# Second attention of layer 1: its node part inside the first attention, one written order for both, norms behind each group

## The chip, the cores and the metric

The kernel runs on one core of a Trainium2 chip. The metric is the device time of one execution in microseconds. TensorE is called PE here, VectorE DVE, ScalarE ACT, GpSimd POOL and SyncE SP.

## The reference

A graph network of four layers over 3125 nodes with 256 features and 103125 edges. The change lies in layer 1, whose graph part has two attentions in a row, the first with four heads, the second with one:

```python
z = jnp.einsum('ni,hoi->nho', h, W1)
es = jnp.einsum('nho,ho->nh', z, a_s)
ed = jnp.einsum('nho,ho->nh', z, a_d)
e = _leaky(es[src] + ed[dst])
alpha = _segment_softmax(e, dst, n)
m = jax.ops.segment_sum(alpha[:, :, None] * z[src], dst, num_segments=n)
h1 = jax.nn.elu(m.reshape(n, HEADS * HID))
z2 = h1 @ W2.T
e2 = _leaky((z2 @ a2[:OUT_DIM])[src] + (z2 @ a2[OUT_DIM:])[dst])
alpha2 = _segment_softmax(e2, dst, n)
out = jax.ops.segment_sum(alpha2[:, None] * z2[src], dst, num_segments=n)
```

The result is added to `x`. Then come a layer norm of `x` and a feed-forward part with a shared network and four gated experts, added to `x` again.

## The kernel before

The edges are not gathered in this layer. Once, early on, the kernel counts how many edges go from each source to each destination and keeps that matrix as bytes (`count_d`). An attention is then a dense product: for a tile of 128 sources, a matrix `pt` of weights is made for a range of destinations, and PE multiplies it with the features `zs` of the sources, a column of ones among them for the softmax's denominator. There are `NS` = 25 source tiles of 128 (the last has 53) and `NT` = 25 destination tiles of `TP` = 125.

The weights come from one DVE instruction, `weigh` (L2066): the maximum of a row `q` of the destination and a scalar `bar` of the source, times the counts. The factor exp(es) of the source lies in `zs`, so the leaky rectifier needs no exponential per edge. The counts come on SP's queue (`count_tile`, L2073), in a ring of four buffers.

**First attention** (`dense`). The destinations are cut into chunks of 6, 6, 6 and 7 tiles. In a chunk, each source tile takes four weighs (one per head, 750 or 875 columns), 16 matmuls into `acc0` and `acc1` (L2321: pairs of heads, two PSUM banks each) and 8 for the sums into `acc2` (L2326). The `pt` ring has 7 buffers. After each source tile the loop runs one piece of side work, `next(work, None)`. Side work of a chunk is what the chunk before left behind: `turned` transposes the accumulators (L2279) and yields, then takes the inverse of the sums (L2285, L2286) and scales on ACT with an exponential for the ELU (L1121, L1123; from tile 18 on a part of it on DVE, L1125), and yields; `finish` (L1130) ends the ELU one tile later. `elu_turned` transposes the result into `xT` (L1141, L1142). Behind the last chunk all its side work runs alone.

The whole of `dense` is inside a manual schedule for PE, DVE and ACT: the instructions of these engines keep the order in which the program writes them. Outside such a block a planner orders each engine's instructions.

**Second attention** (`dense_one`, outside any manual schedule). First the node part, `node_pieces`: row products for `q` (L2012, L2013), and for each source tile two products of 257 columns, a copy by ACT into `zs` (L2027) and a copy by DVE of the source term (L2030). At the end come the exponentials of all source terms (L2032, L2036) and the scaling of all of `zs` (L2041). Then, for each of seven groups of destinations (`GROUPS`: four of 4 tiles, three of 3), 25 source tiles, with one weigh and 4 or 3 matmuls of 257 columns each (L2373), and three DVE instructions per destination tile that add the result to `x` (L2377 to L2379).

**Feed-forward** (`ffn1`). A layer norm per group (L632 to L644), which the planner places as soon as a group of `x` is ready, then for each group transposes of the normed rows into `xT` (`columns`, L294, L300, L302), the gate, and the two networks. Here PE's order alone is written by hand, in a table of steps.

Of the kernel before, what the change touches and what calls it, by code (L numbers as in the profile page):

```python
# [11 lines left out]
F32 = mybir.dt.float32  # L12
# [5 lines left out]
OP = mybir.AluOpType  # L18
# [40 lines left out]
def dview(ap, offset, dims):  # L59
    return bass.AP(tensor=ap.tensor, offset=ap.offset + offset, ap=[list(d) for d in dims])  # L60


class Net:
# [1104 lines left out]
        gw, gb = self.weight(c, "L1_ffn_gW"), self.row(c, "L1_ffn_gb")  # L1168
        return s1, s2, s3, sb1, sb2, e1, e2, e3, eb1, eb2, b3, own, gw, gb

    def ffn1(self, x, xn, xT, weights):
        nc, tc = self.nc, self.tc
        E = 4
        with ExitStack() as s:
# [9 lines left out]
                return nt * TP, slice(t0 * TP, (t0 + nt) * TP)  # L1184

            def columns(i):
                self.transposed(ps, xT, xn, groups=[GROUPS[i]])

            def gate(i):
                nt = GROUPS[i][1]  # L1190
# [54 lines left out]
                            + [(turns[i][:, ts], b3)])  # L1245
                    nc.vector.tensor_add(x[:, t0 + t, :], x[:, t0 + t, :], q)

            for g in GROUPS:
                self.layernorm(xn, x, g)
            steps = ((0, shared1), (1, lambda i: third(i, 0, 2)), (0, lambda i: first(i, 0)), (1, lambda i: third(i, 2, 4)), (0, turn),  # L1250
                     (0, shared2), (0, lambda i: second(i, 0)), (0, lambda i: first(i, 1)), (-1, columns), (0, lambda i: second(i, 1)), (-1, gate))
# [368 lines left out]
class Dense(Net):  # L1620
# [360 lines left out]
    def nodes(self, c, name, H):  # L1981

        HW = C + H
        return (c.tile([P, NS, HW + 31], F32, name="zs"), c.tile([P, NS, H], F32, name="bar"),
                self.dram.tile([H, N], F32, name="q_" + name))
# [57 lines left out]
            if h % 2:  # L2043
                yield

    def dense_nodes(self, c, name, xT, H, slope):
        nodes = self.nodes(c, name, H)
        with self.tc.tile_pool(name="dn", bufs=1) as w, self.tc.tile_pool(name="dnp", bufs=4, space=PSUM) as ps:
            for _ in self.node_pieces(nodes, name, xT, H, slope, w, ps):
                pass  # L2050
        return nodes

    def beside(self, c, name, xT, H, slope, mix, bias=None, gw=None):

        nodes = self.nodes(c, name, H)
# [199 lines left out]
                while ends:  # L2255
                    ends = [e for e in ends if next(e, self) is not self]

    def dense(self, nodes, scaled, then, finish=None, loops=False, early=None):


        nc, tc = self.nc, self.tc
# [1 line left out]
        W = D + 1  # L2263
        zs, bar, q_d = nodes
        with ExitStack() as s:
            wq = s.enter_context(tc.tile_pool(name="daq", bufs=6))
            wa = s.enter_context(tc.tile_pool(name="daa", bufs=4))
            wp = s.enter_context(tc.tile_pool(name="dap", bufs=7))
            wo = s.enter_context(tc.tile_pool(name="dao", bufs=1))
            ps1 = s.enter_context(tc.tile_pool(name="dap1", bufs=1, space=PSUM))  # L2270
            ps = s.enter_context(tc.tile_pool(name="dapp", bufs=2, space=PSUM))

# [20 lines left out]
            def ask(c, i0):  # L2293
                t0, nt = chunks[c]
                d0, n = t0 * TP, nt * TP
                for i in range(i0, i0 + 2):
                    q = wq.tile([P, 875], F32, name="q_head")
                    nc.scalar.dma_start(q[:, :n], dview(q_d, i * N + d0, [[0, P], [1, n]]))
                    queries.setdefault(t0, []).append(q)

            work = iter(())
            with tc.manual_schedule(engines={mybir.EngineType.PE, mybir.EngineType.DVE, mybir.EngineType.Activation}):
                for i in (0, 2):
                    ask(0, i)
                for c, (t0, nt) in enumerate(chunks):
                    d0, n = t0 * TP, nt * TP
                    half = (nt + 1) // 2
                    banks = [(0, half * TP), (half * TP, n)]
                    qs = queries.pop(t0)
                    acc = [ps1.tile([P, 2, 512], F32, name=f"acc{i}") for i in range(3)]  # L2310
                    for t in range(NS):
                        a, K = self.count_tile(wa, t, d0, n, loops)
                        pts = [self.weigh(wp, qs[i][:K, :n], bar[:K, t, i:i + 1], a, n, K) for i in range(4)]
                        st = dict(start=(t == 0), stop=(t == NS - 1))

                        for i0 in (0, 2):
                            for b, (b0, b1) in enumerate(banks):
                                for i in range(i0, i0 + 2):
                                    for f in (0, 32):
                                        r = 64 * (i % 2) + f  # L2320
                                        nc.tensor.matmul(acc[i // 2][r:r + 32, b, :b1 - b0], zs[:K, t, i * W + f:i * W + f + 32],  # L2321
                                                         pts[i][:K, b0:b1], **st)
                        for b, (b0, b1) in enumerate(banks):
                            for i in range(4):
                                z = i * W + D
                                nc.tensor.matmul(acc[2][32 * i:32 * i + 32, b, :b1 - b0],  # L2326
                                                 zs[:K, t, z:z + 32], pts[i][:K, b0:b1], **st)
                        if t == 12 and t0 + nt < NT:
                            ask(c + 1, 0)
                        next(work, None)  # L2330
                    for _ in work:
                        pass
                    if t0 + nt < NT:
                        ask(c + 1, 2)
                    os = []
                    for i, p in enumerate(acc):
                        o = wo.tile([P, 2, 512], F32, name=f"o{i}")
                        for b, (b0, b1) in enumerate(banks):
                            nc.scalar.activation(o[:, b, :b1 - b0], p[:, b, :b1 - b0], AF.Copy)
                        os.append(o)  # L2340
                    work = turned(os, t0, nt, half)
                    if t0 + nt < NT:
                        work = chain(work, then(t0, nt, ps))
                if early:
                    early(ps)
                for _ in work:
                    pass
                work = then(t0, nt, ps)
                if early:
                    return work  # L2350
                for _ in work:
                    pass

    def dense_one(self, x, name, xT, slope):

        nc, tc = self.nc, self.tc
        with ExitStack() as s:
            c = s.enter_context(tc.tile_pool(name="da", bufs=1))
            zs, bar, q_d = self.dense_nodes(c, name, xT, 1, slope)
            q = c.tile([P, N], F32, name="q_all")  # L2360
            nc.scalar.dma_start(q, dview(q_d, 0, [[0, P], [1, N]]))
            wa = s.enter_context(tc.tile_pool(name="daa", bufs=4))
            wp = s.enter_context(tc.tile_pool(name="dap", bufs=6))
            wo = s.enter_context(tc.tile_pool(name="dao", bufs=4))
            ps = s.enter_context(tc.tile_pool(name="dapp", bufs=2, space=PSUM))
            for t0, nt in GROUPS:
                d0, n = t0 * TP, nt * TP
                acc = [ps.tile([TP, C + 1], F32, name=f"acc{i}") for i in range(nt)]
                for t in range(NS):
                    a, K = self.count_tile(wa, t, d0, n, False)  # L2370
                    pt = self.weigh(wp, q[:K, d0:d0 + n], bar[:K, t, :], a, n, K)
                    for i in range(nt):
                        nc.tensor.matmul(acc[i], pt[:K, i * TP:(i + 1) * TP], zs[:K, t, :C + 1],  # L2373
                                         start=(t == 0), stop=(t == NS - 1))
                for i in range(nt):
                    inv = wo.tile([TP, 1], F32, name="inv")
                    nc.vector.tensor_scalar(inv, acc[i][:, C:], 1e-30, None, op0=OP.max)  # L2377
                    nc.vector.reciprocal(inv, inv)
                    nc.vector.scalar_tensor_tensor(x[:, t0 + i, :], acc[i][:, :C], inv, x[:, t0 + i, :],  # L2379
                                                   op0=OP.mult, op1=OP.add)  # L2380

# [674 lines left out]
    def run(self, x_in, out):  # L3058
# [1 line left out]
        self.setup_dense()  # L3060
        pool = self.ctx.enter_context(tc.tile_pool(name="x", bufs=1))
        x = pool.tile([TP, NT, C], F32, name="x")
        self.xn_all = pool.tile([P, NT, C], F32, name="xn")
        xn = self.xn_all[:TP]
        xT = pool.tile([P, KC, N], F32, name="xT")
        x_v = x_in.rearrange("(t p) c -> p t c", p=TP)
# [11 lines left out]
    def layers(self, x, xn, xT, out, late):  # L3078
        nc, tc = self.nc, self.tc
        xn_d = self.dram.tile([N, C], F32, name="xn_d")  # L3080
        with tc.tile_pool(name="hold", bufs=1) as hold:
# [21 lines left out]

                    y_d, (gw1, wkv) = self.routed0(x, xn, xT, xn_d, gate, weights, following)

            with tc.tile_pool(name="da", bufs=1) as c, tc.tile_pool(name="elu", bufs=2) as w:
                nodes = self.beside(c, "g1", xT, 4, 0.01, lambda work: self.mix1(x, xn, xT, work, (y_d, gate[-1]), wkv), gw=gw1)
                pre.close()
                minus = w.tile([P, 1], F32, name="minus", bufs=1)
                nc.gpsimd.memset(minus, -1.0)  # L3110
                scaled, finish = self.elu_parts(w, xn)
                self.dense(nodes, scaled, lambda t0, nt, ps: self.elu_turned(minus, xT, xn, t0, nt, ps), finish)
        with tc.tile_pool(name="ffn1", bufs=1) as wp:
            weights = self.ffn1_weights(wp)
            self.dense_one(x, "g1b", xT, 0.01)
            self.ffn1(x, xn, xT, weights)

        norms = self.ffn2_norms(late.enter_context(tc.tile_pool(name="bn2", bufs=1)))
        right = ExitStack()
# [155 lines left out]
```

## Time and profile before

| what | value |
|---|---|
| median of 3 runs | 5175.78 us (5175.36 to 5178.33) |
| the profiled execution | 5168.58 us |
| its span, first to last instruction | 5166.8 us |
| PE busy in the span | 4686.3 us, 91% |
| DVE | 3403.8 us, 66% |
| ACT | 1659.9 us, 32% |
| POOL | 1522.7 us, 29% |
| mean granted PE clock | 0.943 |
| first attention's weighs (and those of a later layer), L2066 on 750 or 875 columns | 773.3 us of DVE, 800 instructions |
| second attention's matmuls, L2373 | 276.1 us of PE, 1250 records |

Each time is from one profiled execution. A product of 32-bit numbers shows as two records on PE. Busy PE time is modelled from pipelined matmuls; idle time of an engine that limits nothing costs nothing. In the span the first attention of layer 1 begins at 1710.7 us; its last matmuls are issued at 2128.8, the first of the second attention start at 2195.2, its last end at about 2471, and the feed-forward ends at about 2662.

### The profile page before, as it was taken

The numbers are of one execution on the slowest core, as the hardware profiler recorded it, in microseconds if no ns is written. First come the engines' busy times: TensorE is split into PE (matmuls) and PEld (weight loads), VectorE is DVE, ScalarE is ACT, GpSimd is POOL, SyncE is SP. The second block draws the span as 40 slices with busy tenths as digits, with TensorE's granted clock in tenths as the row PEclk, the third lists the DMA queues.
The fourth block names the chain that finished last, engine by engine and source line by source line (L and its number), as shares of the span: only waits on it lengthen the run. The fifth ranks groups of instructions, "written<-read, shape, count | busy, mean of one in ns | idle before, by whom it ended". The sixth has DMA issues, their size and how long they took to land.

```text
span 5166.8 us, 74947 instructions
## 1 busy us (share of the span) xinstructions
PE 4686.3 (91%) x28167; PEld 2876.9 (56%) x28167; DVE 3403.8 (66%) x5802; ACT 1659.9 (32%) x2789; POOL 1522.7 (29%) x1414
## 2 busy tenths in 40 slices
PE   6898999969899899899999999999997788989878
PEld 4564433548656644388555333455664565555567
DVE  6987887755635899555334999622236887777743
ACT  2668877731343011200232011233331102333221
POOL 1107866814300000000001000000005777777733
PEclk8899999979999999899999999999998889999989
DMA  4866544531300111111000111200006566666645
GB/s 94 82 59 167 162 125 142 150 106 64 100 1 1 46 37 40 40 38 35 2 16 1 51 35 38 67 15 0 1 1 171 166 173 186 174 182 179 175 138 172
DMA packets 350161, 443.50 MB, mean 86 GB/s; under 512 B 144857, under 2 KB 269147, under 8 KB 349220
## 3 DMA queue, kind: packets, MB, share of 16 engines
q1 hardware_dynamic: 266674, 222.80, 17.9%
q0 software_dynamic: 55024, 175.53, 11.7%
q10 hardware_dynamic: 28095, 40.29, 2.5%
q8 instruction: 228, 3.74, 0.3%
q14 instruction: 140, 1.15, 0.1%
HBM read 384.87 MB, written 56.78 MB: 85 GB/s over the span
## 4 chain that ended last, share of the span: by engine, by line
PE 67%; DVE 11%; issue 6%; POOL 5%; ACT 4%; DMA 3%; SPq 0%; DVEq 0%; ACTq 0%; POOLq 0%
PE acc L2321 9%; PE p_tr L750 8%; PE acc L2373 5%; PE p_n L2161 5%; PE p_acc L2545 5%; PE acc L2326 4%; PE p_h L750 4%; PE p_y L750 4%; PE p_q L750 4%; POOL z_edge L2477 3%; PE p_f L2206 3%; PE p_a L750 3%; DVE pt L2066 2%; PE p_t L750 2%; PE p_kvt L750 2%
## 5 line engine op out<-in xcount | busy, mean ns | idle before, releaser
L2477 POOL DMA_INDIRECT z_edge<-tab,src_i x806 | 775.4, 962 | 268.4 <-issue 207.1
L2066 DVE SCALAR_TENSOR_TENSOR pt<-q_head,bar,a 128x750 f32<-128x750 f32 (+2 forms) x800 | 773.3, 1028 | 42.9 <-PE acc L2326 27.9
L2321 PE MATMUL acc<-pt,zs 128*32 128x375 f32 (+1 forms) x6400 | 630.0, 496 | 22.7 <-DVE pt L2066 20.3
L2545 PE MATMUL p_acc<-z_edge,oh 128*125 128x264 f32 x2044 | 542.4, 427 | 89.9 <-DVE z_edge L2536 89.8
L2192 POOL TENSOR_TENSOR pt_far<-pt_far,a_far 128x1125 f32<-128x1125 f32 (+1 forms) x200 | 476.3, 2383 | 277.7 <-ACT pt_far L2191 249.7
L2545 PEld LDWEIGHTS p_acc<-z_edge,oh 128*125 128x125 f32 x2044 | 421.8, 210 | 189.8 <-DVE z_edge L2536 98.7
L2147 DVE SCALAR_TENSOR_TENSOR pt<-q_here,bar,a 128x1000 f32<-128x1000 f32 (+1 forms) x384 | 455.9, 1251 | 47.0 <-DMA a<-count_d 16.4
L2161 PE MATMUL p_n<-pt,zs 128*64 128x500 f32 (+1 forms) x1600 | 402.6, 596 | 30.4 <-DVE pt L2147 30.4
L2321 PEld LDWEIGHTS acc<-pt,zs 128*32 128x32 f32 x6400 | 237.0, 109 | 332.9 <-issue 225.5
L2326 PE MATMUL acc<-pt,zs 128*32 128x375 f32 (+2 forms) x3200 | 346.8, 491 | 0.0
L1434 DVE SCALAR_TENSOR_TENSOR x<-p_y,sm,x 125x256 f32<-125x256 f32 x200 | 96.7, 484 | 379.4 <-PE p_y L750 379.4
L2373 PE MATMUL acc<-zs,pt 128*125 128x257 f32 x1250 | 276.1, 383 | 11.8 <-DMA a<-count_d 11.8
L2373 PEld LDWEIGHTS acc<-zs,pt 128*125 128x125 f32 x1250 | 235.1, 189 | 52.9 <-issue 14.6
L2161 PEld LDWEIGHTS p_n<-pt,zs 128*64 128x64 f32 (+1 forms) x1600 | 159.1, 137 | 188.2 <-issue 88.5
L1418 ACT ACTIVATE h<-p_tr,bn 128x500 f32<-128x500 f32 (+1 forms) x224 | 161.5, 723 | 295.0 <-PE p_tr L750 295.0
L2190 ACT ACTIVATE pt_far<-q_log,log_s 128x1125 f32<-128x1125 f32 (+1 forms) x200 | 244.8, 1224 | 19.4 <-PE p_f L2206 17.1
L2206 PE MATMUL p_f<-pt_far,zs 128*64 128x375 f32 (+1 forms) x1200 | 242.6, 486 | 9.1 <-POOL pt_far L2192 9.1
L2536 DVE TENSOR_TENSOR z_edge<-z_edge,near_e 128x2112 f32<-128x2112 f32 (+1 forms) x101 | 236.5, 2342 | 20.4 <-ACT near_e L2528 20.4
L2191 ACT ACTIVATE pt_far<-pt_far,log_s 128x1125 f32<-128x1125 f32 (+1 forms) x200 | 247.0, 1235 | 6.5
L2326 PEld LDWEIGHTS acc<-pt,zs 128*32 128x32 f32 (+1 forms) x3200 | 129.6, 109 | 146.3 <-issue 135.0
L2066 DVE SCALAR_TENSOR_TENSOR pt<-q_all,bar,a 128x500 f32<-128x500 f32 (+3 forms) x175 | 119.2, 683 | 123.1 <-PE acc L2373 120.7
L1165 POOL IOTA own<- 5x256 f32 x1 | 0.4, 355 | 663.2 <-PE acc L2326 663.2
(570 smaller groups left out, 7738.0 us busy)
## 6 DMA issues: line engine op xcount, KB each, us to landing
a<-count_d SPq DMA_DIRECT2D x384, 125.0 KB
a_far<-far_d SPq DMA_DIRECT2D x96, 281.2 KB
row<-dst_row SPq DMA_DIRECT2D x101, 224.0 KB
a<-count_d SPq DMA_DIRECT2D x144, 93.8 KB
ef<-in_edge_s SPq DMA_DIRECT2D x101, 128.0 KB
z_edge<-tab,src_i POOLq DMA_INDIRECT x806
count_d<-stage SPq DMA_DIRECT2D x12, 781.2 KB
q_head<-q_g ACTq DMA_DIRECT2D x24, 375.0 KB
```

Of the source, the lines that this page charges most:

```text
L750: self.nc.tensor.matmul(p, a, b, start=(i == 0), stop=(i == len(pairs) - 1))
L2066: self.nc.vector.scalar_tensor_tensor(pt[:K, :n], q, bar, a[:K, :n], op0=OP.max, op1=OP.mult)
L2147: nc.vector.scalar_tensor_tensor(pt[:K], q[:K], bar[:K, t, h:h + 1], a[:K].rearrange("p (j n) -> p j n", j=2), op0=OP.max, op1=OP.mult)
L2161: nc.tensor.matmul(accs[u][64 * j:64 * j + 64, :M * TP], zs[:K, t, h * W:h * W + 64], pt[:K, j, :], start=(t == 0), stop=(t == NS - 1))
L2191: nc.scalar.activation(f[:K], f[:K], AF.Exp, bias=log_s[:K, 1, t, h], scale=1.0 - 0.2)
L2192: nc.gpsimd.tensor_tensor(f[:K], f[:K], a[:K], OP.mult)
L2206: nc.tensor.matmul(far_accs[u][b][64 * i:64 * i + 64, :n], zs[:K, t, z:z + 64], fs[i][:K, b * n:(b + 1) * n], start=(t == 0), stop=(t == N ...
L2321: nc.tensor.matmul(acc[i // 2][r:r + 32, b, :b1 - b0], zs[:K, t, i * W + f:i * W + f + 32], pts[i][:K, b0:b1], **st)
L2326: nc.tensor.matmul(acc[2][32 * i:32 * i + 32, b, :b1 - b0], zs[:K, t, z:z + 32], pts[i][:K, b0:b1], **st)
L2373: nc.tensor.matmul(acc[i], pt[:K, i * TP:(i + 1) * TP], zs[:K, t, :C + 1], start=(t == 0), stop=(t == NS - 1))
L2477: nc.gpsimd.indirect_dma_start(out=zs[i][:, j, :], out_offset=None, in_=table, in_offset=bass.IndirectOffsetOnAxis(ap=src[:, c0 + j:c0 + j ...
L2545: nc.tensor.matmul(acc[t], ohs[i, t][:, k - a, :], zs[i][:, k - c0, :HW], start=(k == cols[t][0]), stop=(k == cols[t][1] - 1))
```

## The change

1. The node part of the second attention is cut by source tile (`node`). A piece takes two products of 258 columns (the destination term is one of them, so the row products go), two small exponentials on ACT that read the product from PSUM, a DVE copy of the destination term into `eds`, and the scaled copy by ACT into `zs`. The nodes of the tiles that a chunk completed run as further side work of the next chunk. After tiles 10 and 24, `rows` transposes the destination terms and writes `q` to memory.
2. `zs` of the second attention takes the place of the first one's output rows (`xn_flat`).
3. The second attention's loop stands in `go`, inside the manual schedule of `dense`. The last chunk's side work runs in its first group, two pieces per source tile.
4. The layer norm of a group and its transposes (`columns` in `onward`) are side work of the next group; the feed-forward does this for the last group alone (`turned=6`).
5. The weights of the feed-forward are loaded at source tile 14 of the second group.

```diff
-            for g in GROUPS:
+            for g in GROUPS[turned:]:
                 self.layernorm(xn, x, g)
...
-            work = iter(())
+            work = first(wo, ps) if first else iter(())
...
                         if t == 12 and t0 + nt < NT:
                             ask(c + 1, 0)
+                        elif t == 12 and onward:
+                            go = onward(wq, wa, wp, wo, ps1, ps)
                         next(work, None)
...
+                if onward:
+                    return go(chain(work, then(t0, nt, ps)))
...
+        def first(wo, ps):
+            wt = wo.tile([P, 2, 512], F32, name="o2")[:, 0, :].rearrange("p (k f) -> p k f", k=KC)
+            loaded = self.gnn_loads(w, name, 1, wt)
+            yield
+            gws.append(self.gnn_products(loaded, ps, 1, "p_o"))
+            yield
+
+        def node(t, ps):
+            n = min(P, N - t * P)
+            p = ps.tile([P, 512], F32, name="p_o")[:n, :C + 2]
+            self.mm(p, [(xT[:, k, t * P:t * P + n], gws[0][:, k, :]) for k in range(KC)])
+            e = zs[:n, t, C:]
+            nc.scalar.activation(e, p[:, C:C + 1], AF.Exp, bias=shift[:n], scale=1.0)
+            nc.scalar.activation(bar[:n, t:t + 1], p[:, C:C + 1], AF.Exp, scale=slope - 1.0)
+            nc.vector.tensor_copy(eds[:n, t:t + 1], p[:, C + 1:])
+            nc.scalar.activation(zs[:n, t, :C], p[:, :C], AF.Identity, scale=e)
...
+        known = [0]
+        cuts, ready = [0, 11, NS], 17
+
+        def nodes(t1, ps):
+            while known[0] < NS and min((known[0] + 1) * P, N) <= t1 * TP:
+                t = known[0]
+                known[0] += 1
+                node(t, ps)
+                yield
+                if t + 1 in cuts:
+                    rows(cuts[cuts.index(t + 1) - 1], t + 1, ps)
+                    yield
...
+            def columns(i):
+                t0, nt = GROUPS[i]
+                mv = self.moments(x, GROUPS[i])
+                yield
+                rstd = self.norms.tile([TP, 4], F32, name="rstd")
+                nc.scalar.activation(rstd[:, :nt], mv[:, :nt, 1], AF.Sqrt, bias=self.eps5[:TP], scale=1.0)
+                yield
+                nc.vector.reciprocal(rstd[:, :nt], rstd[:, :nt])
...
+                for t in range(nt):
+                    nc.vector.tensor_scalar(out[:, t, :], x[:, t0 + t, :], mv[:, t, 0:1], rstd[:, t:t + 1], op0=OP.subtract, op1=OP.mult)
+                    yield
+                for k in range(KC):
+                    p = ps.tile([P, 512], F32, name="p_o")
+                    for t in range(nt):
+                        nc.tensor.transpose(p[:, t * TP:(t + 1) * TP], out[:, t, k * P:(k + 1) * P], self.ident[:TP, :TP])
+                    nc.scalar.activation(xT[:, k, t0 * TP:(t0 + nt) * TP], p[:, :nt * TP], AF.Copy)
+                    yield
...
+            def go(work):
+                pairs = 0
+                for i, (t0, nt) in enumerate(GROUPS):
...
+                    for t in range(NS):
+                        if t == ready and i == 0:
+                            for _ in work:
+                                pass
+                        a, K = self.count_tile(wa, t, d0, n, False)
+                        pt = self.weigh(wp, q[:K, :n], bar[:K, t:t + 1], a, n, K)
+                        for j in range(nt):
+                            nc.tensor.matmul(accs[j // 2][:TP, j % 2, :C + 1], pt[:K, j * TP:(j + 1) * TP], zs[:K, t, :],
+                                             start=(t == 0), stop=(t == NS - 1))
+                        for _ in range(1 if i else 2):
+                            next(work, None)
+                        if t == 14 and i == 1:
+                            load()
+                        if t == 20 and i + 2 < len(GROUPS):
+                            ask(i + 2)
+                    for _ in work:
+                        pass
+                    for j in range(nt):
+                        acc = accs[j // 2][:TP, j % 2, :]
+                        inv = wo.tile([TP, 1], F32, name="inv_1", bufs=4)
+                        nc.vector.tensor_scalar(inv, acc[:, C:C + 1], 1e-30, None, op0=OP.max)
+                        nc.vector.reciprocal(inv, inv)
+                        nc.vector.scalar_tensor_tensor(x[:, t0 + j, :], acc[:, :C], inv, x[:, t0 + j, :], op0=OP.mult, op1=OP.add)
+                    work = columns(i)
...
-        with tc.tile_pool(name="ffn1", bufs=1) as wp:
-            weights = self.ffn1_weights(wp)
-            self.dense_one(x, "g1b", xT, 0.01)
-            self.ffn1(x, xn, xT, weights)
...
+            self.ffn1(x, xn, xT, weights, len(GROUPS) - 1)
+            f1.close()
```

## Prediction

> **What bounds the kernel now.** I began with the page: PE is busy for 91% of the span and DVE for 66%. Averages hide which stage the change touches, so I then asked for busy time by stretch of the span. The stretches are the four column chunks of the first attention, what lies between the attentions, the second attention, and the feed-forward. The columns are the stretch, its length, the busy time of PE, PE's weight loads, DVE, ACT and POOL, then the granted PE clock, DMA share and GB/s.
>
> ```profile
> core 0: us, PE busy (x) PEld busy (x) DVE busy (x) ACT busy (x) POOL busy (x), PEclk, DMA share, GB/s
> 1710.66:1808.57 97.91, 97.88 (x1200) 71.18 (x1200) 94.92 (x102) 1.71 (x4) 0.00 (x0) 0.97 0.14 38
> 1808.57:1909.00 100.43, 100.43 (x1222) 42.61 (x1222) 94.93 (x117) 15.81 (x57) 0.00 (x0) 1.00 0.14 40
> 2012.00:2128.80 116.80, 116.80 (x1230) 43.13 (x1230) 106.15 (x116) 15.58 (x58) 0.00 (x0) 1.00 0.08 21
> 2128.80:2195.20 66.40, 46.23 (x175) 27.65 (x172) 20.32 (x61) 24.43 (x69) 1.54 (x4) 0.81 0.22 62
> 2195.20:2471.00 275.80, 275.77 (x1250) 235.08 (x1250) 147.48 (x315) 1.78 (x6) 0.00 (x0) 0.99 0.15 35
> ```
>
> In the first attention PE is always busy, but DVE is busy for 91 to 97% of it: two engines are almost equally full. In the second, PE alone is full and DVE works half the time. Between them lie 66.4 us, of which 20.2 us are idle PE at a clock of 0.81. That hole is what the change can win.
>
> Third, DVE's own sequence in order of time, in the last chunk. The bracket is idle time before the group and what ended it.
>
> ```profile
> 2023.13 4.25 DVE L2066 SCALAR_TENSOR_TENSOR pt<-q_head,bar,a 128x875 f32<-128x875 f32 x4
> 2027.29 0.16 DVE L2285 TENSOR_SCALAR inv<-p_o 125x4 f32<-125x4 f32 x1
> 2027.49 0.18 DVE L2286 RECIPROCAL inv<-inv 125x4 f32<-125x4 f32 x1
> 2027.58 3.18 DVE L2066 SCALAR_TENSOR_TENSOR pt<-q_head,bar,a 128x875 f32<-128x875 f32 x3
> 2031.22 1.13 DVE L2066 SCALAR_TENSOR_TENSOR pt<-q_head,bar,a 128x875 f32<-128x875 f32 x1 [0.45 <-PE acc L2326]
> 2032.27 0.42 DVE L1130 SCALAR_TENSOR_TENSOR xn<-elu_e,xn 125x256 f32<-125x256 f32 x1
> ```
>
> The order is exactly the written one: four weighs, then inv and reciprocal, then four weighs, then finish. The scale step follows the weighs of the next source tile because `turned` yields between its transposes and its inv; so DVE asks for a PSUM tile one source tile after PE was told to fill it. The fourth weigh waits for PE (0.45 us): seven `pt` buffers allow DVE a lead of under one source tile.
>
> Last, the waits between the attentions: waiter, awaited, total us, times, longest.
>
> ```profile
> DVE es L2030 <- ACT zs L2027: 29.6, 23, 4.8
> DVE xn L1125 <- ACT elu_e L1121: 11.2, 7, 3.2
> PE acc L2373 <- DMA a<-count_d: 11.8, 1, 11.8
> ```
>
> DVE's small copy waits for ACT's read of the same PSUM tile, every time.
>
> **The change part by part.** Durations: a weigh takes 0.93 us of DVE for 750 columns (four in 3.73), 1.06 for 875, 0.69 for 500, and its result is there 0.07 later. PE needs 3.8 us per source tile for 750 (rows start at 1894.82 and 1898.61), 4.4 for 875, and 0.44 for one product of 257 columns (1250 records in 275.7 us, two per product). Three transposes start-to-start take 0.53, so one is 0.15 to 0.18; small ACT operations 0.20 to 0.23; DVE's copy 0.16.
>
> *Removed:* the stretch from 2128.8 to 2195.2, 66.4 us, and the second attention's 275.7: 342.1 us to 2470.9. With it go seven row products (PE, 14 products at 0.83 or 0.63, 10.4 us), the 6.83 us scaling of all zs, and the clock's recovery.
>
> *Node pieces in the first attention.* Pieces per chunk: 13 for `turned`, 4 for the transposes, then 5, 6 (and one `rows`) and 6 nodes in chunks two, three and four: at most 24 of 25 source tiles, so all fit. PE's own part is two products, 0.87 us each node, 14.8 us for 17. But `node` has no yield: DVE's copy of `eds` sits in the queue before the next four weighs, and needs the product that PE starts only after the present tile's matmuls. What is queued behind the waiting copy is all that PE lives on. From PE's last issue of the product: ACT's first exponential begins 0.3 us later (at 2155.33 four products of 0.87 begin, at 2156.50 ACT reads the first), two take 0.4, the copy ends at 0.9. Weighs land at 1.9, 2.85, 3.75 and 4.7. The first pair of banks needs the first two: 2.85 to 4.1 (two times 0.64). The second pair waits for the fourth: 4.7 to 6.0, and the sums row ends at 7.25. Without a node the same tile takes 3.8, so 3.45 us stall; with 0.87 of product 4.3 per node. At 875 columns the same walk ends at 8.2 against 4.4: 3.8 stall, 4.65 in all. Eleven times 4.3 and six times 4.65 are **+75 us**. Bounds: 14.8 us if DVE kept its lead, 75 us as walked; I take the walk, because the order of DVE rows above is the written order. Walking the unchanged program in this way gives chunks of 98, 100.5, 100.6 and 116.5 us, against 97.9, 100.4, 103 and 116.8 in the rows.
>
> Here the row of DVE's copy waiting for ACT counts 0.4 us per node. The Trainium skill, page "PSUM — Partial Sum Buffer", section "PSUM bank collisions raise a hardware error", says that two engines must be kept apart on a bank even when both only read. By that rule the copy keeps waiting; if readers could overlap, the term would be some 7 us smaller.
>
> *First chunk:* weight loads and four small products in one piece, DVE copying each: 1.8 us of PE and one stall of 2.9, **+4.7**. The loads hide behind the first source tile; uncovered, they cost the 5.9 us that DVE waited for its first counts there.
>
> *Group 0 of the second attention.* Weighs and sums for 500 columns are 0.69 on DVE and 1.76 on PE. Two pieces run per source tile, so for seven tiles the transposes and the scale step stand in one turn, with no weigh between: weigh lands, matmuls 1.8, transposes 0.53, 0.3 to DVE, inv and reciprocal 0.4, 0.1, ACT's exponentials 0.93 (DVE's xn row waits for them, above), xn 0.45, weigh 0.7: 5.2 us where PE has 2.3 of work. Seven are 36.4. Then 2.2 and 2.8 (ELU transposes), 4.9 (one node), three of 5.3 (two nodes, the second copy ending 2.8 after the matmuls), 4.3 (node and rows), and eleven at 1.76: 85.9 against 44.0, **+41.9**. Bounds: 13 us of PE work if all else hid, 60 if the clock falls to half there.
>
> *Group ends.* In the old second attention the weighs of the next group ran before the last sums came out (6 weighs lead at its start). Now the order is fixed: four times 0.79 of DVE begin 1.1 us before PE's end, then the next weigh, 0.7: PE idles 2.9 us (2.4 for three tiles). Four and two: **+16.4**. The moments, 0.575 a tile, stand before the second weigh: idle 1.0 to 1.6 at each of six, **+7.2**. Cover for both would be a weigh ahead of them, which the order lacks; the bound below is 0. Transposes moved in: 48 or 36 small ones by 0.15, **+6.5**. Other norm pieces cost nothing: DVE has 1 us spare per tile. That cover gone, they cost 0.41 each.
>
> *Feed-forward:* loses those 6.5, some 2.4 of waits on its PSUM ring (0.4 at each transposition), and 2.2 at its head, where scores waited for two evictions: **-11**. The norms themselves already lay inside the second attention.
>
> *Queues.* SP now passes a dozen weight loads in group 1 (some 7 us of issue) with four count buffers (7 us of PE) as cover: 0 to 5, I take **+2**. The q rows are written in group 0 and first needed a group later (44 us). ACT's broadcasts and weight issues, about 0.4 each, meet an ACT that is 80% idle: nothing; if not covered, 6 us.
>
> *Sum:* the second attention now takes 275.2 + 41.9 + 16.4 + 7.2 + 6.5 = 347.2 against 342.1, **+5.1**. With 75 + 4.7 - 11 + 2 it is **+76 us**. The profiled execution took 5168.6 us (span 5166.8 and 1.8 around it), 7.2 below the median of 5175.8; so 5244.6 for such an execution, 5252 beside the median, and I say 5250.
>
> **The rivals.** *Faster:* the written order does not hold for the new pieces, and the weighs go ahead of whatever waits, as in the old second attention, where evictions and weighs interleaved freely. Then only PE work is left: 342.1 becomes 275.2 + 13 + 6.5, and the first attention gains 16.6, the loads 2, the feed-forward loses 11: -40, **5136 us**. For it: the old second attention. Against it: that one stood outside a manual schedule, and the new loop is inside. The stalls worked out above are 116 us (60.8 in nodes, 2.9 in the first chunk, 28.9 in group 0, 23.6 at group ends); the sign turns once fewer than 40 of them remain.
>
> *Slower still:* the PE clock. After an idle stretch of 4.03 us, the windows 1659 to 1664 show 0.50; gaps of about 1 us between 1475 and 1485 leave it at 1.00. My gaps are 2 to 2.9 us, between the two. At half clock group 0's seven tiles cost 2.3 more each and six group ends 2 more: +28, **5280 us**.
> The Trainium skill, page "TensorE: Matmul & The Clock Gate", Part 1, puts the fall after about one idle window of 3.4 us; by that rule these gaps cost no clock and the sum stands.
>
> *Half of it:* DVE's lead survives the nodes but not group 0 and the group ends: the 60 us of stall in the chunks vanish, **5191 us**.
>
> **How the numbers follow.** About 0.2% (10 us) is what a measurement here can tell. Stalls as walked 0.67, with slow clock 0.10, half of it 0.05, faster 0.15, and 0.03 that errors cancel to within 10 us. So slower 0.82, same 0.03, faster 0.15. The range leaves out the faster case: 5185 to 5290.
>
> **What would show it.** The chunks two to four grow to about 122, 126 and 144 us, with DVE's copy of `eds` waiting for ACT and PE for `pt` just after it; group 0 takes some 86 us, groups 1 to 3 some 49. If chunks stay at 101 to 122 us, the first step is wrong; if group 0 takes about 57, the second; PE clock under 0.9 in group 0 would be the clock rival.

## Result and the profile after

The change made the kernel slower: 5269.81 us (median of 6 runs, 5262.53 to 5281.19) against 5175.23 us (6 runs, 5166.75 to 5178.33). The ratio is 1.0186, with a 95% interval of 1.0172 to 1.0200: 94.6 us more.

The profiled execution took 5281.19 us, the highest of its runs, with a span of 5279.4 us. That is 112.6 us above the profiled span of before, so I cut both at the same events: the start of the first attention, its first sum, the start of the second attention, its end, the end of the feed-forward (the last two stages overlap by 0.4 us). The last two columns are of two experiments below.

| us | before | after | forecast of the difference | measured | before, once more | three ahead |
|---|---|---|---|---|---|---|
| up to the first attention | 1710.7 | 1719.7 | 0 | +9.0 | 1724.5 | 1717.9 |
| first attention's matmuls | 418.1 | 500.1 | +79.7 | +82.0 | 417.8 | 444.2 |
| from there to the second attention's end | 342.5 | 356.6 | +5.1 | +14.1 | 342.5 | 295.2 |
| feed-forward | 190.6 | 186.7 | -11 | -3.9 | 190.6 | 185.2 |
| the three together | 950.8 | 1043.0 | +76 (2 of it for queues) | +92.2 | 950.5 | 924.2 |
| all behind them | 2505.3 | 2516.7 | 0 | +11.4 | 2501.8 | 2504.6 |

Nearly all that the medians show lies in the three stages that the change touches: 92.2 of 94.6 us. The +9.0 and +11.4 outside are put down to scatter. The unchanged kernel, profiled a second time, also reached the first attention 13.8 us later than in its first profile, and still took 950.5 us for the three stages. What lies behind the stages takes 2501.8 to 2509.8 us in the seven edited versions of the changed kernel below, whose code there is the same.

Here are the windows that answer to those of before: the first chunk, chunks two to four, the seven scale steps at the head of group 0, group 1, and the feed-forward.

```profile
core 0: us, PE busy (x) PEld busy (x) DVE busy (x) ACT busy (x) POOL busy (x), PEclk, DMA share, GB/s
1719.70:1821.40 101.70, 100.35 (x1208) 46.23 (x1208) 94.94 (x104) 1.60 (x4) 0.00 (x0) 0.97 0.16 46
1821.40:1944.50 123.10, 114.46 (x1258) 45.76 (x1250) 96.29 (x123) 20.63 (x75) 0.00 (x0) 1.00 0.13 33
1944.50:2072.80 128.30, 118.06 (x1263) 46.55 (x1255) 95.69 (x123) 20.41 (x78) 0.00 (x0) 1.00 0.12 32
2072.80:2219.87 147.07, 135.65 (x1263) 48.16 (x1255) 108.09 (x123) 20.41 (x77) 0.00 (x0) 1.00 0.09 25
2219.87:2261.00 41.13, 22.89 (x78) 17.92 (x78) 12.01 (x35) 7.45 (x30) 0.35 (x1) 0.79 0.12 31
2313.70:2364.30 50.60, 47.46 (x208) 40.00 (x208) 24.21 (x52) 1.47 (x3) 0.00 (x0) 0.94 0.22 48
2576.40:2762.70 186.30, 182.49 (x611) 96.12 (x611) 71.87 (x322) 62.77 (x104) 0.20 (x2) 0.93 0.00 1
```

DVE's busy time in chunk two, 96.29 us, is what it was before (94.93), but it now fills 78% of a longer window instead of 95%. Both engines have holes. They wait for each other.

DVE's own sequence in chunk three, where each turn now holds a node, shows the place. The bracket is the idle time before a group and what ended it.

```profile
2030.31 0.16 DVE L2378 COPY ed<-p_o 128x1 f32<-128x1 f32 x1 [4.24 <-ACT bar L2377]
2030.39 3.73 DVE L2060 SCALAR_TENSOR_TENSOR pt<-q_head,bar,a 128x750 f32<-128x750 f32 x4
2038.35 0.16 DVE L2378 COPY ed<-p_o 128x1 f32<-128x1 f32 x1 [4.23 <-ACT bar L2377]
2038.43 3.73 DVE L2060 SCALAR_TENSOR_TENSOR pt<-q_head,bar,a 128x750 f32<-128x750 f32 x4
```

DVE stands idle for 4.24 us in front of a copy of 0.16 us, and the four weighs, which PE lives on, stand behind it. PE, in the same time:

```profile
2036.82 1.14 PE L750 MATMUL p_o<-gw_g1b,xT 128*128 128x258 f32 x4
2039.49 3.87 PE L2315 MATMUL acc<-pt,zs 128*32 128x375 f32 x30 [1.53 <-DVE pt L2060]
```

The node's product comes behind the present tile's matmuls. The next tile's matmuls then wait 1.53 us for the first weigh, and 30 of them are spread over 3.87 us (32 take 2.7 where PE is fed) because the weighs now come just in time. One turn takes 8.04 us (2030.31 to 2038.35), where the forecast walked 8.1 and a turn without a node takes 3.8.

The waits from chunk two to four (waiter, awaited, total us, times, longest) name the same wait, once per node:

```profile
DVE ed L2378 <- ACT bar L2377: 76.5, 17, 5.3
```

### The profile page after: what moved, and what is told of

Its sections match the earlier page's. It is cut to its first block, busy times and chain, and to the rows that moved or that the text cites. A ratio compares the mean times of both kernels' runs of the same rounds, so it can differ in the third digit from the quotient of the medians.

```text
span 5279.4 us, 74869 instructions
## 1 busy us (share of the span) xinstructions
PE 4739.4 (90%) x28141; PEld 2865.4 (54%) x28141; DVE 3392.4 (64%) x5793; ACT 1669.3 (32%) x2838; POOL 1522.0 (29%) x1413
## 4 chain that ended last, share of the span: by engine, by line
PE 66%; DVE 13%; issue 6%; DMA 6%; POOL 5%; ACT 4%; ACTq 0%; SPq 0%; DVEq 0%; POOLq 0%
PE acc L2315 9%; PE p_tr L750 8%; PE acc L2450 6%; PE p_acc L2635 5%; PE p_n L2155 4%; PE acc L2320 4%; PE p_y L750 4%; PE p_h L750 4%; PE p_q L750 4%; POOL z_edge L2567 3%; DVE pt L2060 3%; PE p_a L750 3%; PE p_f L2200 3%; PE p_t L750 2%; PE p_kvt L750 2%
## 5 line engine op out<-in xcount | busy, mean ns | idle before, releaser
L2060 DVE SCALAR_TENSOR_TENSOR pt<-q_head,bar,a 128x750 f32<-128x750 f32 (+4 forms) x975 | 888.9, 965 | 119.2 <-PE acc L2450 74.1
L2315 PE MATMUL acc<-pt,zs 128*32 128x375 f32 (+1 forms) x6400 | 661.6, 496 | 54.0 <-DVE pt L2060 43.2
L2315 PEld LDWEIGHTS acc<-pt,zs 128*32 128x32 f32 x6400 | 226.1, 109 | 400.3 <-issue 238.7
L2320 PE MATMUL acc<-pt,zs 128*32 128x375 f32 (+2 forms) x3200 | 364.7, 491 | 0.0
L2450 PE MATMUL acc<-xn,pt 128*125 128x257 f32 x1250 | 299.8, 401 | 41.7 <-DVE pt L2060 41.7
L2450 PEld LDWEIGHTS acc<-xn,pt 128*125 128x125 f32 x1250 | 243.8, 198 | 90.8 <-DVE pt L2060 31.4
L750 PE MATMUL p_tr<-h,w_W 128*128 128x500 f32 (+1 forms) x448 | 188.7, 566 | 3.7 <-ACT h L1419 2.1
L750 PE MATMUL p_tr<-xT,w_W 128*128 128x500 f32 (+1 forms) x448 | 181.9, 548 | 7.0 <-ACT h L1419 7.0
```

The costliest lines, as they stand in the source:

```text
L750: self.nc.tensor.matmul(p, a, b, start=(i == 0), stop=(i == len(pairs) - 1))
L2060: self.nc.vector.scalar_tensor_tensor(pt[:K, :n], q, bar, a[:K, :n], op0=OP.max, op1=OP.mult)
L2320: nc.tensor.matmul(acc[2][32 * i:32 * i + 32, b, :b1 - b0], zs[:K, t, z:z + 32], pts[i][:K, b0:b1], **st)
L2450: nc.tensor.matmul(accs[j // 2][:TP, j % 2, :C + 1], pt[:K, j * TP:(j + 1) * TP], zs[:K, t, :], start=(t == 0), stop=(t == NS - 1))
```

## Experiments

**Theory:** the loss is one of order. In the node, DVE's copy of a product's last column stands ahead of the weighs in DVE's queue. In the second attention, a tile's weigh stands behind the side work of the turn before, and behind the previous group's sums. PE's added work is small. **Rivals:** PE's added products and transposes are the price themselves, or the two engines' reads of one PSUM tile are. Each would leave most of the loss in place when only the order is changed.

### The copy on ACT

```diff
-            nc.vector.tensor_copy(eds[:n, t:t + 1], p[:, C + 1:])
+            nc.scalar.activation(eds[:n, t:t + 1], p[:, C + 1:], AF.Copy)
```

> The copy of eds goes from DVE to ACT, nothing else. Theory (DVE's queue stands still behind this copy, and the weighs behind it): chunks two to four of the first attention fall from 123, 128 and 147 us to about 105, 108 and 122, group 0 of the second attention from 94 to about 86, in all about 5200 us. Rival (the added products themselves, PSUM traffic or the PE clock cost the time): DVE is relieved of 25 copies of 0.16 us, so 5265 to 5270 us and chunks as they are.

Measured: 5211.8 us, ratio to before 1.0061 (1.0045 to 1.0078), against 1.0186 for the whole change. In the profile, the first attention's matmuls take 444.9 us instead of 500.1. Of this kernel, a line of DVE's sequence in chunk three, the window of chunk two, and PE's sequence in chunk three:

```profile
2012.20 3.73 DVE L2060 SCALAR_TENSOR_TENSOR pt<-q_head,bar,a 128x750 f32<-128x750 f32 x4 [1.27 <-PE acc L2320]
```
```profile
1823.20:1930.90 107.70, 107.70 (x1256) 45.24 (x1253) 96.03 (x118) 20.46 (x79) 0.00 (x0) 1.00 0.14 38
```
```profile
2012.11 1.14 PE L750 MATMUL p_o<-gw_g1b,xT 128*128 128x258 f32 x4
...
2017.11 1.14 PE L750 MATMUL p_o<-gw_g1b,xT 128*128 128x258 f32 x4
```

PE is busy for all of its 107.70 us, and it is now DVE that waits for PE (1.27 us a turn). The turn takes 5.00 us (2012.11 to 2017.11) instead of 8.04. A turn without a node takes 3.8. So of the 4.24 us that a node added to a turn, 3.04 were the wait and 1.2 are PE's work on it: the first rival holds for somewhat over a quarter. Group 0 gained less than expected: it takes 90.6 us instead of 93.9 (86 was expected), at a granted clock of 0.83 there instead of 0.88.

### The copy kept on DVE, a piece later

The node's product stays where it was; what reads it is issued with the next piece. All engines keep their work.

```diff
-                node(t, ps)
+                new = node(t, ps)          # the product alone
+                if held:
+                    stored(*held.pop())    # ACT's exponentials, DVE's copy, the scaled copy
+                held.append(new)
                 yield
...
```

> All of a node but its two products is written one piece later; every instruction is kept on its engine. Theory: in the chunks DVE's copy then asks for a product that PE finished a source tile before, so they fall as with the copy on ACT (105, 108, 122 us); in group 0, with two pieces per turn, less is won; about 5205 us. Rival (the copy itself or the reads of one PSUM tile by two engines cost the time): within 10 us of 5270.

Measured: 5218.25 us, ratio 1.0073 (1.0056 to 1.0090), in line with the run before, and 13 us above what was expected: the second attention did not gain (356.5 us).

```profile
1823.50:1931.20 107.70, 107.70 (x1255) 45.37 (x1257) 97.00 (x123) 20.60 (x74) 0.00 (x0) 1.00 0.14 38
```

Chunk two takes the same 107.7 us, with the copy still on DVE and both engines still reading one PSUM tile. Over the whole first attention this edit saves 51.3 us (448.8 instead of 500.1), the copy on ACT 55.2. So neither the engine nor the shared tile was more than a small part of the cost; the copy's place in the queue was nearly all of it.

### The weighs one source tile ahead

```diff
+                ahead = weights(0, 0)
...
-                        pt = self.weigh(wp, q[:K, :n], bar[:K, t:t + 1], a, n, K)
+                        pt, K = ahead
                         ...
+                        if t + 1 < NS:
+                            ahead = weights(i, t + 1)
+                        elif i + 1 < len(GROUPS):
+                            ahead = weights(i + 1, 0)
                         for _ in range(1 if i else 2):
                             next(work, None)
```

> In the second attention each weigh is written one source tile earlier, ahead of the side work and of the sums at a group's end. Theory: group 0 falls from 94 to about 66 us, the other groups lose the 3.5 us of idle PE at their start (50 to about 46.5), in all 45 to 50 us: about 5222. The chunks stay at 123, 128 and 147. Rival (a clock at half, or count tiles that land late, sets group 0): group 0 stays above 85 and the whole above 5250.

Measured: 5220.44 us, ratio 1.0076 (1.0059 to 1.0092). The first attention is as slow as in the changed kernel (498.2 us), and the second, which took 356.6, now takes 310.2. PE's sequence in group 0 (of this kernel), then its window for the second attention:

```profile
2225.78 2.00 PE L2455 MATMUL acc<-xn,pt 128*125 128x257 f32 x8 [0.42 <-DVE pt L2060]
...
2228.55 2.00 PE L2455 MATMUL acc<-xn,pt 128*125 128x257 f32 x8 [0.44 <-DVE pt L2060]
```
```profile
2218.10:2528.30 310.20, 295.85 (x1366) 245.67 (x1362) 155.08 (x351) 25.72 (x78) 0.35 (x1) 1.00 0.18 40
```

A scale step's turn takes 2.77 us (2225.78 to 2228.55), group 0 takes 60.5 us instead of 93.9, and the other groups of four tiles 47.1 instead of some 50. The clock is 1.00 over the whole stage.

### Both

The copy on ACT and the weighs one source tile ahead, each edited as above:

```diff
-            nc.vector.tensor_copy(eds[:n, t:t + 1], p[:, C + 1:])
+            nc.scalar.activation(eds[:n, t:t + 1], p[:, C + 1:], AF.Copy)
...
-                        pt = self.weigh(wp, q[:K, :n], bar[:K, t:t + 1], a, n, K)
+                        pt, K = ahead
```

> Copy on ACT and weighs one source tile ahead. Theory: the two gains lie in different stages but for the nodes of group 0, so they add: about 5155 us, some 20 below the kernel before the change. Rival (PE is the bound once DVE waits less, and the transposes and nodes that moved under it are no gain): 5175 us or more.

Measured: 5167.68 us (8 runs), ratio 0.9975 (0.9964 to 0.9986). The first edit alone had brought the ratio down by 1.25%, the second by 1.10%, and both together do by 2.11%, a little less than the sum, and the time is 13 us above the one expected: the two waits are nearly independent. With them gone, the change is a small gain.

### The kernel before, once more

The kernel before without any edit, as a measure of how far single executions differ.

> The kernel before the change once more, for a second profile of it. In the first one the counting stage ended at 382 us of the span and the first attention began at 1710.7; in the five profiles since at 390 to 393 and 1719.7 to 1723.2, though nothing of that stage was edited. If that is scatter of single executions, this profile begins the attention near 1720 too; if the changed storage moved it, near 1711.

Measured: 5182.24 us, ratio 1.0001 (0.9990 to 1.0012). Its profile is a column of the table above: single executions differ by 10 us outside the stages of the change, and by 0.3 us within them.

### The norms where they were

To the version with both edits, so that the norms of the feed-forward follow the second attention as before:

```diff
-                    work = columns(i)
+                    work = iter(())
...
-            self.ffn1(x, xn, xT, weights, len(GROUPS) - 1)
+            self.ffn1(x, xn, xT, weights)
```

> Copy on ACT and weighs one ahead, but the norms and transposes of all groups are back in the feed-forward. Theory (they are worth little: PE work that only moves, and norms that lay under the second attention anyway): the second attention falls from 310 to about 302 us, the feed-forward grows from 180 to about 193, since the first norms now stand alone; in all 5168 to 5178 us against 5168 with them. Rival (the norms behind each group are the part that pays): 5185 us or more.

Measured: 5164.22 us (10 runs), ratio 0.9971 (0.9961 to 0.9982), not to be told from 0.9975 (0.9964 to 0.9986). The second attention and the feed-forward, with both edits first, without the norms inside after it:

```profile
2167.10:2477.10 310.00, 295.78 (x1366) 245.44 (x1362) 154.65 (x343) 25.96 (x86) 0.35 (x1) 1.00 0.18 40
2477.10:2656.90 179.80, 175.56 (x611) 92.90 (x611) 72.24 (x324) 63.04 (x104) 0.53 (x3) 0.96 0.00 1
```
```profile
2165.60:2470.70 305.10, 291.44 (x1322) 242.91 (x1318) 151.50 (x343) 19.31 (x74) 0.35 (x1) 0.99 0.19 41
2470.70:2659.00 188.30, 181.70 (x655) 98.38 (x655) 76.05 (x330) 65.69 (x110) 0.54 (x3) 0.96 0.00 1
```

The second attention gains 4.9 us and the feed-forward loses 8.5; the 3.6 us between them do not show in the medians. With the weighs ahead, this part of the change is worth nothing that could be measured.

### One piece per turn in group 0

From the changed kernel, without the two other edits:

```diff
-                        for _ in range(1 if i else 2):
+                        for _ in range(1):
```

> The changed kernel with one piece of side work per source tile in the first group, not two; what is left runs at source tile 17. Theory (transposes and scale step in one turn stop DVE with no weigh between): group 0 falls from 94 to about 68 us, chunks and other groups stay, in all about 5245 us. Rival (half clock or too much work in that group): group 0 stays above 85 us, 5260 or more.

Measured: 5244.44 us, ratio 1.0129 (1.0111 to 1.0148). The second attention falls from 356.6 to 332.4 us, all of it in group 0 (69.4 us instead of 93.9). PE's sequence in group 0:

```profile
2223.37 2.00 PE L2450 MATMUL acc<-xn,pt 128*125 128x257 f32 x8 [0.86 <-DVE pt L2060]
2225.20 0.49 PE L2273 MATMUL p_o<-ident,o 128*125 128x128 f32 x3
2225.53 1.90 PE L2450 MATMUL acc<-xn,pt 128*125 128x257 f32 x8
2228.28 2.00 PE L2450 MATMUL acc<-xn,pt 128*125 128x257 f32 x8 [0.85 <-DVE pt L2060]
```

With one piece per turn a weigh stands between a tile's transposes and its scale step, and PE waits 0.86 us once in two turns instead of 2.6 us in every turn: two source tiles take 4.91 us (2223.37 to 2228.28), as long as one turn with both pieces took at full clock. More turns with side work, and still 24 us less: it is not the amount of side work that cost, but two dependent pieces in one turn. Some 7 of the 24 us had been lost to a lower clock, as shown below.

### Copy on ACT, and the weighs three source tiles ahead

As in the version with both edits, but a list of three weighs is kept ahead, across the ends of the groups. `weights(k)` appends the weigh of step k, counted over all groups.

```diff
+                for k in range(3):
+                    weights(k)
...
-                        pt = self.weigh(wp, q[:K, :n], bar[:K, t:t + 1], a, n, K)
+                        pt, K = ready_pts.pop(0)
                         ...
+                        weights(i * NS + t + 3)
                         for _ in range(1 if i else 2):
                             next(work, None)
```

> Copy on ACT, and weighs three source tiles ahead, over the group ends too. With one ahead the first groups still take 47.1 us, where the matmuls and transposes need 45.2, and the seven scale steps 2.77 where PE has 2.3. Theory: both gaps close, 11 and 3 us, so about 5154 us. Rival (a further wait, on counts or on PE's order, stands there): 5165 or more.

Measured: 5150.09 us (6 runs, 5146.45 to 5155.43), ratio 0.9944 (0.9931 to 0.9957): faster than both kernels.

```profile
2162.10:2457.30 295.20, 292.18 (x1366) 245.62 (x1362) 154.17 (x341) 25.91 (x86) 0.36 (x1) 1.00 0.19 42
```

PE is busy for 292.18 of 295.20 us: the second attention, with the rest of `turned`, the nodes and the norms in it, now costs 19.4 us more than its matmuls alone did before (275.8), and the stretch of 66.4 us between the attentions is gone. Against that stand the 26.1 us by which the first attention grew (444.2 against 418.1). In its profile the three stages take 924.2 us against 950.8.

## Why the prediction was right, and where its sizes were off

The sign, the mechanism and the places were as forecast. The forecast of 5250 was 20 us short, 16 of them in the three stages.

**Node pieces and the first chunk: right.** They were put at +79.7 us and measured +82.0. The walk of one turn (8.1) is the row of 8.04; the first chunk added 4.1 for 4.7 (from the start to the first eviction). Chunks two to four, counted from first eviction to first eviction, take 123.1, 128.3 and 146.3 us for "about 122, 126 and 144". The split inside the term was a little off: PE's own part of a node was counted as two products of 0.44, 0.87 us, and runs at 1.2; the wait is then 3.04 instead of 3.45. The two errors nearly cancel, and that the term came within 3 us is in part luck. The bound of 14.8 us for "DVE kept its lead" would have been some 20 (17 times 1.2); with the copy out of the way, the first attention grew by 25.8 to 30.7 us in all (443.9 to 448.8 against 418.1). One reading beside the sum was off too: the row products that went run at 0.89 and 0.68 us each in their rows (a pair from 2159.00 to 2160.77 and from 2169.88 to 2171.23), not at 0.83 and 0.63; no term rests on it.

The forecast let the copy wait 0.4 us for ACT's reads of the same PSUM tile. The Trainium skill's page "PSUM — Partial Sum Buffer", section "PSUM bank collisions raise a hardware error", asks that two readers of a bank be kept apart. This program does so: the copy waited for ACT all 17 times. No run here shows two reads of a bank at once. But the copy one piece later, which still waits for ACT, shows that this wait costs little once no weigh stands behind it: chunk two takes 107.7 us with the copy on either engine.

**Group 0: too small, and by the clock.** Forecast 85.9 us; measured 90.8, which is 93.9 from its first matmul to that of group 1 less 3.1 of idle at the group's end. The step that failed is the flat 5.2 us for each of seven scale steps, which took their gaps as free for the clock. Here is PE's sequence, and the windows of the granted clock around it:

```profile
2224.71 2.00 PE L2450 MATMUL acc<-xn,pt 128*125 128x257 f32 x8 [2.59 <-DVE pt L2060]
...
2229.63 2.88 PE L2450 MATMUL acc<-xn,pt 128*125 128x257 f32 x8 [2.59 <-DVE pt L2060]
...
2235.76 3.79 PE L2450 MATMUL acc<-xn,pt 128*125 128x257 f32 x8 [2.61 <-DVE pt L2060]
```
```profile
2231.00:2235.00 4.00, 2.15 (x7) 1.54 (x5) 0.71 (x4) 0.93 (x4) 0.00 (x0) 0.50 0.00 1
2235.00:2239.00 4.00, 3.24 (x8) 2.58 (x9) 1.04 (x3) 0.00 (x0) 0.00 (x0) 0.50 0.08 16
```

The wait is the one walked, 2.6 us every time, and at full clock a step takes 4.92 us (2224.71 to 2229.63). That is less than the 5.2 of the walk. But in the next two steps the clock is granted at 0.50, eight products take 3.79 us instead of 2.00, and a step takes 6.1 and 7.0. Behind five of the seven gaps of 2.6 us they take 2.88 to 3.79. The seven steps add up to 41.1 us (2219.80 to 2260.93) where 36.4 were forecast and 34.4 would do at full clock: those 4.7 us are nearly all of the term's error of 4.9. The first attention, which had waits of 1.5 us, kept a clock of 1.00.

The forecast weighed the Trainium skill's page "TensorE: Matmul & The Clock Gate", Part 1, by which the clock falls after about one idle window of 3.4 us, so that gaps of 2 to 3 us would cost none. The gaps of 2.6 us measured here did cost clock, and so did the single gaps of the next paragraph, so the measurement decides against that reading. A later section of the page, "A second HAM failure mode: psum-queue depth-cycling", tells of a kernel whose short, frequent idle times made the clock swing; that is nearer to the rows of group 0, but not to single gaps.

**Group ends and moments: right in the first wait, wrong in what follows it.** PE's wait behind a group was put at 2.9 us for four tiles and 2.4 for three. The six such waits make 17.9 us for the forecast 16.4, the longest 3.2:

```profile
PE acc L2450 <- DVE pt L2060: 17.9, 6, 3.2
```

For the moments a second wait of 1.0 to 1.6 us was forecast in each group, 7.2 us in all. None shows. Instead PE ran the first source tiles of each group at half clock. Here are PE's start of group 2, then windows around the starts of groups 3 and 5:

```profile
2364.34 5.95 PE L2450 MATMUL acc<-xn,pt 128*125 128x257 f32 x20 [3.19 <-DVE pt L2060]
```
```profile
2411.51:2418.34 6.83, 4.78 (x11) 3.82 (x12) 6.59 (x20) 0.30 (x1) 0.00 (x0) 0.50 0.13 28
2418.34:2462.71 44.37, 42.23 (x198) 35.89 (x196) 18.32 (x35) 1.18 (x2) 0.00 (x0) 1.00 0.15 34
2503.67:2507.08 3.41, 3.41 (x10) 2.43 (x9) 3.31 (x11) 0.30 (x1) 0.00 (x0) 0.50 0.22 42
```

Each of the six gaps (2.70 to 3.19 us) brought 3.4 or 6.8 us at 0.50, though PE had been busy for some 20 us or more before it. From a group's first matmul to its first transposes, six or seven source tiles, the six groups together take 74.4 us, where the pace of their later tiles (1.735 us for four products, 1.30 for three) gives 61.1. These 13.3 us stand where 7.2 were forecast. With the weighs one source tile ahead no gap over 1.3 us is left in the stage, and the clock stays at 1.00.

Groups 1 to 3 take 50.6, 49.2 and 50.1 us for "some 49". Groups 1 to 6 together took 262.7 us (2313.7 to 2576.4), where 347.2 less 85.9 and less 2.9, or 258.4, were forecast. Of the missing 4.3, the starts of the groups make 6.1, and the other terms take 1.8 back. With the 5.1 of group 0 and its end, less 0.4 because the replaced stage measures 342.5 us and not the 342.1 of the forecast, that is the second attention's +14.1 instead of +5.1.

**The clock rival: true in part.** It asked for 28 us, 2.3 in each of seven steps and 2 at each of six group ends. Beyond the forecast the two places cost 4.7 and 6.1, somewhat over a third of that. The sign that the prediction named for it, a clock under 0.9 in group 0, appeared: 0.88 from 2219.80 to 2313.70. The measured time lies nearer to the 5280 of this rival than to 5250, though a good part of the rest is the feed-forward's.

**Feed-forward: too hopeful.** Put at -11, measured -3.9 in the changed kernel. The feed-forward's code is the same in six of the experiments and takes 179.8 to 185.2 us in them (186.7 in the changed kernel): the seven average 183.4, 7.2 less than before. The -11 is what the best of them shows. The clock is 0.93 in the changed kernel's window and 0.96 in the best one's, and PE's busy time, for the same 611 records, is 182.5 and 175.6 us: that is the 6.9 us between the two. Why the clock fell more often for equal code was not settled.

**Queues:** put at +2. The second attention's waits name only 0.9 us for counts in groups 1 to 6 (3 times, all of DVE and none of PE), so the term was 1 at most.

**The rivals.** "Faster" rested on weighs that go ahead of whatever waits. The chip did not do that by itself: the order of DVE's rows is the written one. When the weighs were written ahead, the price moved as that rival said, but less far: 29 us faster (0.56%) instead of 40. By that rival the first attention was to grow by 16.6 us; it grew by 26.1. "Half of it" is excluded by the chunks, "errors cancel" by the 94.6 us.

## What to carry to other kernels

When work is woven into a loop whose order is fixed, look at what stands behind each new instruction in its engine's queue. Anything that reads a result of PE belongs one piece later than the product, and the feed of the engine that sets the pace belongs ahead of everything that may wait: here nearly the same work in another order was 2.4% of the whole kernel apart (1.0186 against 0.9944). Two pieces that depend on each other should not share a turn, and an idle hole is worth filling only as far as the filled-in work's own time on the full engine is less than the hole.

## What was unexpected of the hardware

- PE gaps of 2.6 to 3.2 us cost clock, and equal gaps did not cost the same. Behind seven gaps of 2.6 us, with about 2.3 us of matmuls between them, the granted clock was 0.50 in some of the steps and 1.00 in others. Behind six single gaps of 2.70 to 3.19 us it was 0.50 every time.
- The clock's changes in that stage (2230.6 to 2544.6) all lie on one grid of 3.41 us, and its stretches at 0.50 last 3.4, 6.8 or 10.2 us. So where a gap falls on the grid may decide what it costs; the rows here do not give the rule.
- With gaps of 0.86 us every two turns (one piece per turn) the clock was 0.99 over group 0 (2218.45 to 2287.88 of that kernel); with gaps of at most 1.3 us (weighs one source tile ahead) it was 1.00 over the whole second attention.
- Two products of 258 columns cost 1.2 us of PE between the first attention's matmuls (128x32 weights). In a long row of them they had cost 0.87, and so they did in group 0 between matmuls of 257 columns (two nodes in 1.74 us, 2188.88 to 2190.62 with the weighs three ahead).
- Two profiles of the same unchanged kernel reached the first attention 13.8 us apart, and then took 950.8 and 950.5 us for the next three stages: spans of two profiled executions are to be compared stage by stage.
